# A band's side work in a scan layer: input rows scaled on GpSimd, and three pieces moved by a slot

## The chip, the cores and the metric

The kernel runs on one core of a Trainium2 chip. The metric is the device time of one execution in microseconds; of several runs the median is given.

## The reference, cut to what matters

The network has four layers on four images of 64 x 64 pixels and 128 channels. The change touches only the first layer, a selective scan in four directions. Cut to the parts that are spoken of:

```python
x = x + L0(_gn(x), ...)                       # group norm, then the layer
# L0:
xh, z = jnp.split(x @ in_proj_w.T, 2, axis=-1)   # 128 -> 2 x 256 channels
z  = silu(z)                                     # the "gates"
xc = silu(depthwise_conv_3x3(xh) + conv_b)
# four directions k over xc: delta, B, C from products of xc, then for each of 4096 positions
h = exp(delta * A) * h + (delta * u) * B         # 256 channels x 16 states
y = sum_n h[n] * C[n]
# the four results are added, and
y = layernorm(y) * out_norm_w + out_norm_b
return (y * z) @ out_proj_w.T
```

The group norm is a per-channel scale `s_` and offset `o_` for each image; "scaling the rows" means applying them to the input.

## The kernel before, in words

**Units and slots.** The first layer is a list of 128 units: 4 images x 4 directions x 8 chunks of 512 positions. A unit has 16 slots, one for each state `n` (the loop at L687). In every slot GpSimd forms `dB` (128 x 1024, L699), ScalarE two `dA` (128 x 512, L704), VectorE two scans `h` (L705), and `transposed()` (L536) gives TensorE eight transposes of an older unit's `h` into `pt` (L549) and eight products into `yT` (L584), and ScalarE the copy `hT` of `pt` (L559). The lag is seven slots. `pt` has one PSUM buffer, `dA` three, `dB` three. The order on TensorE, ScalarE, VectorE and GpSimd is the order in which the code issues (`manual_schedule`, L656); SyncE, which issues nearly all DMAs, is not in that list.

**Preparing the next unit.** `TABLE` (L612) puts the small steps that make the next unit's `delta` and `du` into slots 6 to 12: two products `dp`, four ScalarE passes, VectorE's `delta` (L484) in slots 9 and 11, and GpSimd's `du` (L487) in slots 10 and 12.

**Side work.** Beside the scan of one image, `before()` (L295) makes the next image's convolution and gates, and `after()` (L367) finishes the previous image. Both are generators; each `yield` names a need, and the loop at L741 lets a generator go on when the slot is in the need's set in `SIDE` (L626) and the piece is due. `later(place, f, slots=k)` puts an instruction into a place of the slot `k` slots on: "dve" ahead of the scans, "act0" and "act1" behind the first and the second scan, "act2" behind `hT`.

The side work of a band of 512 positions takes three units when convolutions are due. In this text they are called unit A, B and C:

- Unit A: the second gates' product `zp` in slot 1 (need "z"), its three ScalarE passes `e` in slots 2, 3 and 4, the product on VectorE in slot 5 (`silu`, L344). The previous image's product of `yg` and `z` on GpSimd in slot 7 (L414). The first convolution, nine taps of `cv` (L159), from slot 11 on, one tap a slot.
- Unit B: the convolution ends in slot 3, its passes are in 4, 5 and 6. The second convolution starts in slot 11. For `after()`, in the time of images 1 and 2 only, need "t" comes in slot 12 (`nb`, L388), the small product `mb` of 128 x 4 on VectorE in slot 14 (L390), and the four normalisations `yf` of 128 x 256 on ScalarE (L393) in slots 14 and 15 and in slots 0 and 1 of unit C. `xw`, a copy with transposed order (L362), is in slot 13.
- Unit C: the next band's rows `xn` (128 x 640) are scaled on ScalarE in slot 1 (L326, called by L341). The convolution ends in slot 3, its passes are in 4, 5 and 6. The band's transposes `pg` (L406, need "m") are in slots 11 and 12, their copies `yg` (L408) in 12 and 13, another `xw` in 13, the first gates' product `zp` in 13, and its passes in 14, 15 and in slot 0 of the next unit A.

`pg`, `zp`, `cv` and `dp` share one PSUM bank by way of `spare` (L501). In the time of image 0 there is no `after()`, so `mb`, `yf`, `pg` and `yg` are missing from the three units. In the time of image 3 there is no `before()`, and `after()` takes another form (need "n", normalisation on VectorE).

Of the kernel before, what the change touches and what calls it, by code (L numbers as in the profile page):

```python
# [12 lines left out]
AF = mybir.ActivationFunctionType  # L13
ALU = mybir.AluOpType
# [10 lines left out]
NCH = NT // CH  # L25
# [57 lines left out]
def layer0(sh, A, x_in, x_out, scr, ahead):  # L83
# [6 lines left out]
    tc, nc = sh.tc, sh.nc  # L90
    with ExitStack() as ctx:
# [76 lines left out]
        def grown(b, c, s, pm, later, e=None, gather=None):  # L168
            bias = conv_b[:, s : s + 1], conv_nb[:, s : s + 1]
            xo = silu(pm, *bias, scr(f"xr{b % 2}")[s, :, c * CH : (c + 1) * CH], later, (("act0", 2), ("act0", 3), 4), e)  # L170
            later("act0", gather or by_columns, xo, scr(f"xw{b % 2}")[s], c, slots=10)

        def gates(b, c, v, bank, later, es=(None, None)):
            for s in range(2):
                yield "z"
                zp = bank("zp")
                nc.tensor.matmul(zp, lhsT=w_in[:, 2 + s, :], rhs=v, start=True, stop=True)
                silu(zp, 0.0, 0.0, scr(f"z{b % 3}")[s, :, c * CH : (c + 1) * CH], later, (("act0", 2), ("act0", 3), 4), es[s])
# [126 lines left out]
        def before(b, bank, later):  # L305

            st = small.tile([P, NCH, 6], F32, name="gn_st")
            for c in range(NCH):  # L310
                yield "l"
                t = tmp.tile([P, CH], F32, name="xs", tag="t2", bufs=4)
                nc.sync.dma_start(t.rearrange("p (h w) -> p h w", w=64), A["x_t"][b, :, 8 * c + 1 : 8 * c + 9, 1:65])
                yield "s"
                later("dve", nc.vector.bn_stats, st[:, c, :], t)
            yield "m"
            s_, o_ = sh.group_scale(st, psm, small, "m", exp_rstd)

            def load(c):
                xn = tmp.tile([P, 10, 66], F32, name="xn", bufs=3)  # L320
                nc.sync.dma_start(xn, A["x_t"][b, :, 8 * c : 8 * c + 10, :])
                return xn

            def scaled(xn, c, r0, r1):
                inner = xn[:, max(r0, int(c == 0)) : min(r1, 10 - int(c == NCH - 1)), 1:65]
                nc.scalar.activation(inner, inner, AF.Identity, scale=s_, bias=o_)  # L326

            yield "l"
            ahead = load(0)
            yield "x"  # L330
            later("act2", scaled, ahead, 0, 0, 10)
            for c in range(NCH):
                xn = ahead
                yield from gates(b, c, xn[:, 1:9, 1:65], bank, later)
                for s in range(2):
                    for t, piece in enumerate(conv(xn, s, bank, out := [])):
                        yield piece
                        if c < NCH - 1 and (s, t) == (0, 0):
                            ahead = load(c + 1)
                        if c < NCH - 1 and s == 1 and t == 5:  # L340
                            later("act2", scaled, ahead, c + 1, 0, 10)  # L341
                    grown(b, c, s, out[0], later)

        def silu(v, bias, minus, dst, later, wait, e=None):  # L344
# [22 lines left out]
        def after(b, st, later, bands):  # L367

            for c in bands:
                yield "l"  # L370
                rows = slice(c * CH, (c + 1) * CH)
                if kept:
                    y = kept.pop()
                else:
                    y = tmp.tile([P, 4, 2 * P], F32, name="yf", tag="t4", bufs=4)
                    nc.sync.dma_start(y, tiles(scr(f"y2{b % 2}")[rows, :]))
                z = tmp.tile([P, 2, CH], F32, name="zf", tag="t4", bufs=4)
                nc.sync.dma_start(z, scr(f"z{b % 3}")[:, :, rows].rearrange("s p t -> p s t"))
                mv = small.tile([P, 4, 2], F32, name="ln_mv")
                for q in range(4):  # L380
                    nc.vector.bn_aggr(mv[:, q, :], st[:, 4 * c + q])

                rs = small.tile([P, 4], F32, name="ln_r")
                later("act1", nc.scalar.activation, rs, mv[:, :, 1], AF.Ln, bias=sh.eps5)
                if b + 2 < NB:
                    yield "t"
                    nb = small.tile([P, 4], F32, name="nb")
                    nc.scalar.activation(nb, rs, AF.Exp, scale=-0.5)  # L388
                    mb = small.tile([P, 4], F32, name="mb")
                    later("dve", nc.vector.scalar_tensor_tensor, mb, mv[:, :, 0], -1.0, nb, ALU.mult, ALU.mult, slots=2)  # L390
                    for q in range(4):
                        norm = dict(scale=nb[:, q : q + 1], bias=mb[:, q : q + 1])
                        later("act2", nc.scalar.activation, y[:, q, :], y[:, q, :], AF.Identity, slots=2 + q, **norm)  # L393
                else:
                    yield "n"

                    nb = spare("nb")[:, 0:4]
                    nc.scalar.activation(nb, rs, AF.Exp, scale=-0.5)
                    for q in range(4):
                        later("dve", normed, y[:, q, :], mv[:, q, 0:1], nb[:, q : q + 1])  # L400
                yg = tmp.tile([P, 2, CH], F32, name="yg", bufs=2)
                for s in range(2):
                    yield "m"
                    pt = spare("pg")
                    for q in range(4):
                        nc.tensor.transpose(pt[:, q * P : (q + 1) * P], y[:, q, s * P : (s + 1) * P], sh.ident)  # L406
                    norm = dict(scale=on_w[:, s : s + 1], bias=on_b[:, s : s + 1])
                    later("act0", nc.scalar.activation, yg[:, s, :], pt, AF.Identity, **norm)  # L408
                yield "f"
                xr = tmp.tile([P, 4, DM], F32, name="xr", tag="t2", bufs=4)  # L410
                nc.sync.dma_start(xr, tiles(x_in(b)[rows, :]))
                if b < NB - 1 or c > 2:
                    yield "g"
                nc.gpsimd.tensor_tensor(yg, yg, z, ALU.mult)  # L414
                if b + 2 < NB:
                    yield "o"
                    op = psy.tile([P, 2, 2 * P], F32, name=f"yT{int(not rev)}").rearrange("p r d -> p (r d)")
                else:
                    yield "m"
                    op = spare("op")  # L420
                op = op.rearrange("p (q d) -> p q d", q=4)
                for q in range(4):
                    for s in range(2):
                        nc.tensor.matmul(
                            op[:, q, :], lhsT=yg[:, s, q * P : (q + 1) * P], rhs=w_out[:, s, :], start=(s == 0), stop=(s == 1)
                        )
                later("dve", residual, b, rows, xr, op, slots=2)
# [134 lines left out]
        def products(G, q, hT):  # L562
# [61 lines left out]
            (12, "pool"): ("du1",),  # L624
        }
        SIDE = dict(  # L626
            m={0, 1, 2, 4, 5, 11, 12, 13, 14, 15},
            x={0, 1, 4, 5, 11, 12, 13, 14, 15},
            n={0, 1, 2, 3, 4, 11, 12, 14, 15},
            z={13, 1},  # L630
            c={11},
            g={7},
            s={11, 12, 13, 14, 15, 0, 1, 2, 3},
            t={11, 12, 15, 0},
            o={8},
            f=(),
            l=(),
# [3 lines left out]
        slot = 0  # L641

        def later(place, f, *a, slots=1, **kw):

            todo.setdefault((slot + slots, place), []).append(lambda: f(*a, **kw))  # L645
# [10 lines left out]
        with tc.manual_schedule(engines=order):  # L656
# [4 lines left out]
            for i, (b, k, c) in enumerate(units):  # L661
# [25 lines left out]
                for n in range(NS):  # L687
                    slot = NS * i + n
                    g, q = divmod(n, 4)
# [39 lines left out]
                    if n == 10:  # L729
                        y = unit["y"] = tmp.tile([P, 4, 2 * P], F32, name="y", tag="t4", bufs=4)  # L730
# [15 lines left out]
                        d.step()  # L746
                    for d in sides:
                        if d.need == "t" and n in SIDE["t"] and d.due(slot) and (inside or not any(o.taps for o in sides)):
                            d.free_at = slot + 6
                            d.step()  # L750
                        if d.need == "o" and n in SIDE["o"] and d.due(slot - 8):
                            d.step()
                        if d.need == "s" and n in SIDE["s"] and d.due(slot):
                            d.step()
                        if d.need in ("f", "l") and d.due(slot):
                            if d.need == "l":
                                d.free_at = slot + 3
                            d.step()
# [1455 lines left out]
```

## Time and profile before

| | |
|---|---|
| median of 3 runs | 7645.87 us (7638.12 to 7647.14) |
| the profiled execution's own time | 7645.85 us |
| its span from first to last instruction | 7644.1 us |
| mean granted TensorE clock | 0.966 |
| the scans of the first layer, from first to last | 112.8 to 5594 us |
| units of image 0, 1, 2, 3 begin at | 112.8, 1480.7, 2865.8, 4249.0 us |

The profile's page gives busy time by engine, the chain of waits that ended last, and groups of instructions by source line. In the timeline each row is one instruction or several merged ones: start, length, engine, line, operands, count, and in brackets the idle time of the engine just before and what ended it. Idle times below about 0.15 us are merged away. A row's length can overlap the next row's, since an engine starts its next instruction before the last has drained; the distance between two starts, the pitch, is what an instruction costs its engine.

### The profile page before, as it was taken

Reading aid. Unit: us, or ns where it says so; the run is one execution under the profiler, and the core shown is the slowest. Engines: PE = TensorE matmul, PEld = TensorE weight load, DVE = VectorE, ACT = ScalarE, POOL = GpSimd, SP = SyncE. Lnnn points to the kernel's source line nnn. Section 1 sums busy time; section 2 is a strip of 40 time slices with the busy share of each in tenths; the row PEclk is TensorE's granted clock in tenths of the full one; section 3 lists DMA queues with packets and bytes.
Section 4 is the critical chain, followed back from the end, with each engine's and each line's share of the span. In section 5 each row is a group of like instructions: output and inputs, shape, how many; then the busy total and the mean of one; then the engine's idle time right before and its main releaser. Section 6 shows DMA issues by size and latency. Waiting matters only on the chain.

```text
span 7644.1 us, 140402 instructions
## 1 busy us (share of the span) xinstructions
PE 6293.8 (82%) x52604; PEld 3973.6 (52%) x52604; DVE 6715.7 (88%) x7999; ACT 6135.0 (80%) x9771; POOL 5691.9 (74%) x2688
## 2 busy tenths in 40 slices
PE   7888888778898877888887777787789978686889
PEld 3554444444455544445554444454467756464556
DVE  7999999999999999999999999999956655656678
ACT  7999999999999999999999999999943323324667
POOL 4999999999999999999999999999920024123233
PEclk8999999999999999999999999999999988788999
DMA  6656566546667554565756445555533241331332
GB/s 181 171 177 176 182 175 180 171 154 178 198 180 195 184 179 160 167 196 178 183 191 180 165 169 180 179 185 174 190 92 73 59 120 46 83 99 46 102 95 82
DMA packets 1328925, 1160.66 MB, mean 152 GB/s; under 512 B 718709, under 2 KB 1119697, under 8 KB 1261298
## 3 DMA queue, kind: packets, MB, share of 16 engines
q1 hardware_dynamic: 1323970, 1149.24, 50.4%
q8 instruction: 414, 6.78, 0.4%
q10 hardware_dynamic: 4272, 2.43, 0.1%
q14 instruction: 269, 2.20, 0.1%
HBM read 958.19 MB, written 189.21 MB: 150 GB/s over the span
## 4 chain that ended last, share of the span: by engine, by line
ACT 36%; PE 31%; DVE 18%; issue 8%; POOL 3%; DMA 2%; SPq 1%; ACTq 0%; DVEq 0%; POOLq 0%
ACT hT L559 14%; ACT dA L704 14%; DVE h L705 12%; PE pt L549 5%; PE cv L159 3%; POOL dB L699 3%; PE yT L584 3%; PE pf L939 2%; PE po L952 1%; ACT e L645 1%; ACT delta L478 1%; PE yT L458 1%; PE pz L1183 1%; PE pt L1892 1%; ACT delta L481 1%
## 5 line engine op out<-in xcount | busy, mean ns | idle before, releaser
L705 DVE TENSOR_TENSOR_SCAN h<-dA,state,dB 128x512 f32<-128x512 f32 x4096 | 4927.0, 1266 | 120.7 <-ACT dA L704 72.4
L699 POOL TENSOR_TENSOR dB<-du,Bb 128x1024 f32<-128x1024 f32 x2048 | 4816.5, 2387 | 152.3 <-DVE h L705 118.2
L549 PE MATMUL pt<-ident,h 128*128 128x128 f32 x16384 | 2216.7, 278 | 859.2 <-ACT hT L559 833.8
L704 ACT ACTIVATE dA<-delta,A_neg 128x512 f32<-128x512 f32 x4096 | 2765.5, 696 | 102.7 <-DVE h L705 77.0
L549 PEld LDWEIGHTS pt<-ident,h 128*128 128x128 f32 x16384 | 1802.7, 141 | 1917.7 <-ACT hT L559 1700.5
L559 ACT COPY hT<-pt 128x1024 f32<-128x1024 f32 x2048 | 2080.7, 1016 | 125.5 <-PE pt L549 105.9
L584 PE MATMUL yT<-hT,W 128*32 128x256 f32 x16384 | 1378.6, 409 | 4.3 <-DVE xr L433 3.5
L584 PEld LDWEIGHTS yT<-hT,W 128*32 128x32 f32 x16384 | 456.2, 150 | 346.3 <-issue 324.3
L159 PE MATMUL cv<-xn,taps 128*128 128x512 f32 x936 | 527.1, 645 | 2.7 <-DVE delta L484 2.6
L1183 POOL TENSOR_TENSOR xg<-xg,so 128x1024 f32<-128x1024 f32 x16 | 39.3, 2469 | 622.8 <-PE pu L1183 622.2
L1930 POOL TENSOR_TENSOR S<-S,sm 128x784 f32<-128x784 f32 x128 | 191.1, 1493 | 416.3 <-DVE sm L1928 250.0
L487 POOL TENSOR_TENSOR du<-delta,u 128x512 f32<-128x512 f32 x256 | 327.8, 1281 | 163.6 <-DVE delta L484 162.2
L475 PE MATMUL dp<-xd,w_dt 65*128 65x512 f32 x512 | 288.7, 646 | 33.8 <-DVE delta L484 23.7
L458 PE MATMUL yT<-u,w_x 128*48 128x512 f32 x508 | 244.4, 604 | 21.3 <-DVE y L600 20.1
L1937 ACT ACTIVATE S<-S,mx 128x196 f32<-128x196 f32 x512 | 227.9, 448 | 33.2 <-DVE mx L1964 32.7
L159 PEld LDWEIGHTS cv<-xn,taps 128*128 128x128 f32 x936 | 139.2, 188 | 180.5 <-issue 160.4
L940 ACT ACTIVATE h<-pf,b 128x512 f32<-128x512 f32 x128 | 87.6, 687 | 118.8 <-PE pf L939 100.5
L484 DVE SCALAR_TENSOR_TENSOR delta<-delta,dp 128x512 f32<-128x512 f32 x256 | 169.7, 663 | 3.2 <-ACT delta L481 1.0
L1183 POOL TENSOR_TENSOR WX<-wr,Xs 128x544 f32<-128x544 f32 x40 | 59.3, 1483 | 149.1 <-issue 63.4
L1892 PE MATMUL pt<-ident,S 128*98 128x128 f32 x1024 | 165.6, 286 | 3.5 <-POOL S L1930 2.0
L481 ACT ACTIVATE delta<-delta 128x512 f32<-128x512 f32 x256 | 164.5, 643 | 0.0
L478 ACT ACTIVATE delta<-dp 128x512 f32<-128x512 f32 x256 | 152.3, 595 | 10.4 <-PE dp L475 9.2
(381 smaller groups left out, 6921.7 us busy)
## 6 DMA issues: line engine op xcount, KB each, us to landing
Bb<-l_B SPq DMA_DIRECT2D x512, 1024.0 KB
W<-l_W SPq DMA_DIRECT2D x512, 256.0 KB
l_y<-y SPq DMA_DIRECT2D x127, 512.0 KB
u<-l_xr SPq DMA_DIRECT2D x64, 512.0 KB
u<-l_xw SPq DMA_DIRECT2D x64, 512.0 KB
y<-l_y SPq DMA_DIRECT2D x56, 512.0 KB
V<-l_v SPq DMA_DIRECT2D x512, 49.0 KB
y<-l_y SPq DMA_DIRECT2D x80, 256.0 KB
```

Of the source, the lines that this page charges most:

```text
L159: nc.tensor.matmul(pm, lhsT=taps[:, s, t, :], rhs=xn[:, dy : dy + 8, dx : dx + 64], start=(t == 0), stop=(t == 8),)
L458: nc.tensor.matmul(bank["x"], lhsT=w_x[:, s, k, :], rhs=u[:, s, :], start=(s == 0), stop=(s == 1))
L475: nc.tensor.matmul(bank[s], lhsT=w_dt[:, k, s * P : (s + 1) * P], rhs=xd, start=True, stop=True)
L481: nc.scalar.activation(delta[:, s, :], delta[:, s, :], AF.Ln, bias=1.0)
L487: nc.gpsimd.tensor_tensor(du[:, s, :], delta[:, s, :], u[:, s, :], ALU.mult)
L549: nc.tensor.transpose(pt[:, j, s, :], G["h"][:, s, t0 : t0 + 32, :].rearrange("p t n -> p (t n)"), sh.ident)
L559: return lambda: nc.scalar.copy(hT, pt.rearrange("p j s d -> p j (s d)"))
L584: nc.tensor.matmul(U["yT"][e][32 * jo : 32 * jo + 32, qo % 2, :], lhsT=U["Ws"][G["g"]][:, :, 4 * q + j], rhs=hT[:, j, :], start=((e, jo) n ...
L699: nc.gpsimd.tensor_tensor(dB, du, B_now[:, q : q + 1, :].to_broadcast([P, 2, CH]), ALU.mult)
L704: nc.scalar.activation(dA, delta[:, s, :], AF.Exp, scale=A_neg[:, k, s, n : n + 1])
L705: nc.vector.tensor_tensor_scan(h[:, s, :, q], dA, dB[:, s, :], state[:, s, n : n + 1], ALU.mult, ALU.add)
L1892: nc.tensor.transpose(pt[:, half, hp, :], U["S"][:, e, hp, 98 * half : 98 * half + 98], sh.ident)
```

## The change

The scaling of a band's rows goes from ScalarE to GpSimd and from slot 1 of unit C to slot 8 of unit B, seven slots and one unit boundary earlier (`s == 0, t == 8` is reached in slot 3, and five slots are added). The scaling of an image's first band also goes to GpSimd. The small product and the four normalisations come one slot later (15, then 15, 0, 1, 2). Need "m" loses slot 11, so the transposes of unit C are in slots 12 and 13 and their copies in 13 and 14. The gates' products go from slots 13 and 1 to 14 and 2, and with them their passes and VectorE products. Need "t" keeps only slot 12, which is the one that it has now in the time of images 1 and 2, and its generator waits seven slots instead of six.

```diff
             def scaled(xn, c, r0, r1):
                 inner = xn[:, max(r0, int(c == 0)) : min(r1, 10 - int(c == NCH - 1)), 1:65]
-                nc.scalar.activation(inner, inner, AF.Identity, scale=s_, bias=o_)
+                nc.gpsimd.tensor_scalar(inner, inner, s_, o_, ALU.mult, ALU.add)
...
-                        if c < NCH - 1 and s == 1 and t == 5:
-                            later("act2", scaled, ahead, c + 1, 0, 10)
+                        if c < NCH - 1 and s == 0 and t == 8:
+                            later("act2", scaled, ahead, c + 1, 0, 10, slots=5)
...
-                    later("dve", nc.vector.scalar_tensor_tensor, mb, mv[:, :, 0], -1.0, nb, ALU.mult, ALU.mult, slots=2)
+                    later("dve", nc.vector.scalar_tensor_tensor, mb, mv[:, :, 0], -1.0, nb, ALU.mult, ALU.mult, slots=3)
...
-                        later("act2", nc.scalar.activation, y[:, q, :], y[:, q, :], AF.Identity, slots=2 + q, **norm)
+                        later("act2", nc.scalar.activation, y[:, q, :], y[:, q, :], AF.Identity, slots=3 + q, **norm)
...
-            m={0, 1, 2, 4, 5, 11, 12, 13, 14, 15},
+            m={0, 1, 2, 4, 5, 12, 13, 14, 15},
...
-            z={13, 1},
+            z={14, 2},
...
-            t={11, 12, 15, 0},
+            t={12},
...
-                            d.free_at = slot + 6
+                            d.free_at = slot + 7
```

## The prediction, made before the run

> **What bounds the kernel now.** I read the page first: the share of busy time, the chain, and the groups of the first layer.
>
> ```profile
> PE 6293.8 (82%) x52604; PEld 3973.6 (52%) x52604; DVE 6715.7 (88%) x7999; ACT 6135.0 (80%) x9771; POOL 5691.9 (74%) x2688
> ACT 36%; PE 31%; DVE 18%; issue 8%; POOL 3%; DMA 2%; SPq 1%; ACTq 0%; DVEq 0%; POOLq 0%
> L705 DVE TENSOR_TENSOR_SCAN h<-dA,state,dB 128x512 f32<-128x512 f32 x4096 | 4927.0, 1266 | 120.7 <-ACT dA L704 72.4
> L699 POOL TENSOR_TENSOR dB<-du,Bb 128x1024 f32<-128x1024 f32 x2048 | 4816.5, 2387 | 152.3 <-DVE h L705 118.2
> ```
>
> The chain names ScalarE and TensorE, but over the first layer VectorE is busy some 97% of the time (1346.6 of 1385 us in image 1's part, by the busy times by stretch). So VectorE's scans are the bound and the rest of the chain is what makes them wait. All that can be won lies in VectorE's idle time, mostly `h` waiting for `dA`. The waits of images 1 and 2 (1480 to 4250 us) say so:
>
> ```profile
> DVE h L705 <- ACT dA L704: 49.5, 97, 1.0
> POOL du L487 <- DVE delta L484: 77.6, 59, 2.1
> PEld zp L177 <- ACT yg L645: 13.8, 14, 1.0
> ```
>
> Next, ScalarE's and VectorE's timelines around the steps that move, in a band of image 1 (unit C from 2001.28 us):
>
> ```profile
> 2003.79 1.01 ACT L559 COPY hT<-pt 128x1024 f32<-128x1024 f32 x1
> 2004.69 0.61 ACT L645 ACTIVATE yf<-yf,mb,nb 128x256 f32<-128x256 f32 x1
> 2005.19 0.92 ACT L326 ACTIVATE xn<-xn,gn_o,gn_s 128x640 f32<-128x640 f32 x1
> 2006.01 1.30 ACT L704 ACTIVATE dA<-delta,A_neg 128x512 f32<-128x512 f32 x2
> ...
> 1995.19 1.45 DVE L645 SCALAR_TENSOR_TENSOR mb<-ln_mv,nb 128x4 f32<-128x4 f32 x1
> 2006.80 9.66 DVE L705 TENSOR_TENSOR_SCAN h<-dA,state,dB 128x512 f32<-128x512 f32 x8 [0.71 <-ACT dA L704]
> 2038.20 1.28 DVE L705 TENSOR_TENSOR_SCAN h<-dA,state,dB 128x512 f32<-128x512 f32 x1 [0.88 <-ACT dA L704]
> 2039.80 2.46 DVE L705 TENSOR_TENSOR_SCAN h<-dA,state,dB 128x512 f32<-128x512 f32 x2 [0.31 <-ACT dA L704]
> 2042.43 2.46 DVE L705 TENSOR_TENSOR_SCAN h<-dA,state,dB 128x512 f32<-128x512 f32 x2 [0.17 <-ACT dA L704]
> ```
>
> Two bursts make VectorE wait: the fourth `yf` together with `xn` in slot 1 (0.71), and `yg`, `xw`, `yg` in slots 12 and 13 (0.88, 0.31 and what follows). And `mb`, four elements wide, holds VectorE for 1.45 us.
>
> The pitches, from these timelines: two `dA` 1.22, `hT` 0.91, so a bare slot costs ScalarE 2.13 us; `yf` adds 0.50, `e` 0.50, `yg` 0.66, `xw` 0.97, `xn` 0.82. Two scans cost VectorE 2.35, a product beside them 0.58. TensorE with a tap of `cv` needs 2.53 a slot (`cv` begins at 2085.44 and 2087.97).
>
> Last, busy time by stretch. Columns: length, PE, PEld, DVE, ACT, POOL.
>
> ```profile
> 710.54:728.38 17.84, 17.01 (x127) 9.72 (x125) 16.85 (x14) 16.83 (x24) 17.84 (x8) 1.00 1.10 225
> 668.20:685.93 17.73, 16.90 (x127) 9.83 (x126) 17.11 (x15) 15.86 (x23) 17.73 (x8) 1.00 0.73 242
> 2126.09:2143.53 17.44, 15.91 (x114) 8.96 (x114) 16.69 (x16) 17.40 (x27) 16.44 (x8) 1.00 1.16 259
> 2160.68:2190.80 30.12, 22.17 (x196) 13.44 (x192) 28.30 (x26) 30.01 (x44) 28.94 (x15) 1.00 0.55 160
> ```
>
> The first is slot 14 of B to slot 5 of C in image 0's time, with `xn`; the second the same slots of A to B, without `xn`; the third is B to C in image 1, `xn` beside `yf`; the fourth slot 11 of C to slot 6 of A in image 1.
>
> **What the Trainium skill says.** "SBUF — State Buffer", Who interferes with whom: a VectorE instruction with two SBUF inputs and a GpSimd one that reads SBUF exclude each other for a whole instruction. `mb` fits: in all 16 cases it ends within 0.05 us of the end of the running `dB` in the two timelines. L430, also two SBUF inputs, takes 0.47 us beside a running `dB`, so the rule isn't general here. "ScalarE: Activation LUTs", What ACT_TABLE_LOAD costs: 186 + 0.833 N ns plus 93 per pointer operand, 93 overlapping; for N = 640 that is 0.81, and the pitch of `xn` is 0.82. "GPSIMD Engine Reference", 4.1 Engine selection: one-input work is roughly at line rate. In the trace a copy of 128 x 640 takes 0.84 us (L248), but TENSOR_SCALAR 3.01 us for 1024 elements.
>
> **The change part by part.**
>
> (1) `xn` leaves ScalarE. In image 0's time it is almost hidden: TensorE's nine taps need 2.53 a slot anyway. The stretch with it is 17.84, the one without 17.73, mean difference over five bands 0.11; with the waits around it I take 0.15. There are 7 such bands, and in images 1 and 2 two more without `yf` beside: 9 x 0.15 = 1.4 us. In 12 bands (six an image) `yf` stands beside it. There ScalarE is busy 17.40 of 17.44 and VectorE idles 0.75 to 1.16, mean 0.98. Afterwards ScalarE needs 2.63 in slots 15, 0, 1, 2 and 2.13 in slot 3. When the scans of slot 15 begin it is 0.7 ahead now; without the `yf` of slot 14 about 1.0, since TensorE's 2.53 takes part of the 0.5. Four slots at 2.63 - 2.35 = 0.28 use up 1.1, and slots 3 and 4 then wait for TensorE as they do in unit B. I leave 0.33 idle: 12 x 0.65 = 7.8 us.
>
> (2) `pg`, `yg`, `zp` and `e` one slot later. The same passes, but `xw` now meets the first `yg`, with the reserve of a free slot 12 behind it, and unit A's `e` begin in slot 3 instead of 2, so that slot 2 lets ScalarE recover. Slot by slot for image 1 from slot 12 of C to slot 5 of A, ScalarE's need against VectorE's plus its reserve: before 2.54, 3.76, 2.63, 2.65, 2.96, 2.37, 2.35, 2.61, 2.96, 2.96 (the distances between the scans' starts, mean of five bands, sum 27.8). After: 2.35, 3.26 (reserve 0.5 off 3.76), 2.79, 2.63, 2.65, 2.93, 2.35, 2.35, 2.63, 3.42, sum 27.4. So 0.4 less, in 14 bands: 5.6 us. In image 0's time only `zp` moves: 0.25 by the same count, 7 bands, 1.8 us. TensorE's new waits (the second `pg` for the first `yg`, one shared bank) end before the next `hT` would let it go on: `yg` ends 2.4 us into the slot, `pg` takes 0.66, `hT` ends at 3.8. Behind them stand `pt` and `zp`; without that cover, up to 1.0 us a band.
>
> (3) An image's first band: `zp` waited for `xn` in slot 1 (VectorE idle 0.37 and 0.47 at 1616.39 and 1618.14). With GpSimd ahead and `zp` a slot later I take 0.8 for images 1 and 2, 0.3 for image 0: 1.9 us.
>
> (4) `xn` on GpSimd. Price between 0.84 (the copy) and 1.88 us (3.01 x 640/1024); I take 1.88, the same operation. It stands behind `dB` of slot 8, ahead of two `dB` and `du`. There GpSimd waits anyway:
>
> ```profile
> 2105.18 2.38 POOL L699 TENSOR_TENSOR dB<-du,Bb 128x1024 f32<-128x1024 f32 x1 [0.28 <-DVE h L705]
> 2108.18 2.38 POOL L699 TENSOR_TENSOR dB<-du,Bb 128x1024 f32<-128x1024 f32 x1 [0.63 <-DVE h L705]
> 2111.91 1.28 POOL L487 TENSOR_TENSOR du<-delta,u 128x512 f32<-128x512 f32 x1 [1.34 <-DVE delta L484]
> ```
>
> That is 2.25 us, and 0.24 + 0.63 + 1.09 = 1.96 in image 0's bands. Cost nothing at both ends. Its rows were loaded tens of us before; SyncE's loads don't move with it. Without this cover each us would reach `dB` of slot 13, which is ready only 0.3 us ahead in image 0's time.
>
> (5) `mb` a slot later. It ends when GpSimd's `dB` ends, and GpSimd runs without gaps from `du` on, 2.34 a `dB` against VectorE's 2.35 a slot. So the scans of slot 15 begin at the same boundary as now: the wait of 1.35 us stays, bounds -0.3 and +0.3 x 16; I take 0. SyncE's stores of the gates follow their products by a slot; `W` loads behind them are used slots later: 0.
>
> (6) Image 3's `pg` and `op` from slot 11 to 12: TensorE idles 0.3 to 0.9 a slot there; 0, bounds -1.5 and +1.5.
>
> Sum: 1.4 + 7.8 + 5.6 + 1.8 + 1.9 = 18.5 us. The profiled execution took 7645.85 us, the median is 7645.87; so 7627.4, said as 7627.
>
> **Rivals.** *TensorE takes over* in the 12 bands too, as in image 0's: (1) gives 12 x 0.15 + 1.4 = 3.2, (2) half, 3.7, (3) 1.9: 7637. For it: 2.53 a slot under the taps. Against: TensorE idles 1.5 us in the third stretch. *GpSimd becomes late*: if the two scalar operations cost a pass each, `xn` takes 3.8; 1.8 too much in 7 bands (less 0.3 of lead) and 1.55 in 14, where `mb` passes the later boundary on in full: 10.5 + 21.7 = 32, so 7646 - 18.5 + 32 = 7659, slower. It decides from 1.96 us on. Against: the row of 3.01. *All of ScalarE's relief arrives*: half of the idle time that I leave in the 14 bands (1.83 - 0.4 + 0.33, half of it 0.9) goes too, 13 us more: 7614.
>
> **Chances.** Forecast 0.58 (7617 to 7637, terms half to one and a half), TensorE 0.20, GpSimd 0.12, all relief 0.10. A measurement of this kernel tells about 0.2%, 15.3 us, from no change; the forecast lies just beyond it, two thirds of its case faster (0.40), with the last case 0.50; TensorE and the other third 0.37 the same; slower 0.13 with some of it for mishaps. The range 7608 to 7645 leaves out the slow rival and little else.
>
> **What would show it.** Right: no `xn` on ScalarE, one of about 1.9 us on GpSimd ahead of a shortened wait of `du`; VectorE's wait in slot 1 of C gone, that in slot 13 still near 0.9; `mb` still ended by `dB`; units of image 3 unchanged. Wrong: `dB` late in slot 13, or `mb` of another length, since a changed phase between GpSimd and VectorE would outweigh the small terms.

## The result, and the profile after

| | before | after |
|---|---|---|
| median of 14 runs each | 7643.74 us (7638.12 to 7651.99) | 7630.74 us (7625.07 to 7634.70) |
| ratio, 95% interval | | 0.998 (0.9974 to 0.9987) |
| span of the profiled execution | 7644.1 us | 7630.5 us |
| the scans of the first layer end at | 5594.3 us | 5584.7 us |

The change makes the kernel 13 us faster by the medians. That is 0.17%, at the edge of what the prediction called measurable, though the interval leaves out a ratio of 1. The forecast was 18.5 us.

From the page of the changed kernel, the lines that answer to those shown of before: busy time, shares of the chain, the scans and `dB`.

```profile
PE 6285.6 (82%) x52604; PEld 3974.8 (52%) x52604; DVE 6715.5 (88%) x7999; ACT 6117.9 (80%) x9747; POOL 5707.3 (75%) x2712
ACT 38%; PE 35%; DVE 16%; issue 7%; POOL 2%; DMA 2%; SPq 1%; ACTq 0%; DVEq 0%; POOLq 0%
L705 DVE TENSOR_TENSOR_SCAN h<-dA,state,dB 128x512 f32<-128x512 f32 x4096 | 4927.8, 1266 | 113.7 <-ACT dA L704 60.8
L699 POOL TENSOR_TENSOR dB<-du,Bb 128x1024 f32<-128x1024 f32 x2048 | 4816.4, 2390 | 120.9 <-DVE h L705 91.1
```

ScalarE has 24 instructions fewer and GpSimd 24 more. The scans' wait for `dA` fell from 72.4 to 60.8 us. GpSimd's wait for `h` fell by 27.1, from 118.2 to 91.1 us; 24 rows at 0.88 us are 21 of that. What one of them costs GpSimd, from the instructions on the tile `xn` (least, median, most ns), and how it stands in slot 8 of a unit B, from GpSimd's timeline:

```profile
L326 POOL TENSOR_SCALAR xn<-xn,gn_s,gn_o x24: 822/880/972, 333.9 to 3864.8; 128x640 f32<-128x640 f32 x18, 128x576 f32<-128x576 f32 x6
```

```profile
1964.28 7.05 POOL L699 TENSOR_TENSOR dB<-du,Bb 128x1024 f32<-128x1024 f32 x3
1971.31 0.90 POOL L326 TENSOR_SCALAR xn<-xn,gn_s,gn_o 128x640 f32<-128x640 f32 x1
1972.15 4.78 POOL L699 TENSOR_TENSOR dB<-du,Bb 128x1024 f32<-128x1024 f32 x2
1978.27 1.28 POOL L487 TENSOR_TENSOR du<-delta,u 128x512 f32<-128x512 f32 x1 [1.33 <-DVE delta L484]
```

0.88 us in the median (0.90 in the mean of the 18 with 640 elements), not the 1.88 taken. The two waits of 0.28 and 0.63 ahead of `dB` are used up, and the wait of `du` for `delta` is still 1.33.

Next VectorE's timeline of the same band, from the end of unit B on; unit C begins at 1997.13, its slot 12 at 2028.78.

```profile
1993.59 1.25 DVE L645 SCALAR_TENSOR_TENSOR mb<-ln_mv,nb 128x4 f32<-128x4 f32 x1
1994.76 16.94 DVE L705 TENSOR_TENSOR_SCAN h<-dA,state,dB 128x512 f32<-128x512 f32 x14
...
2026.41 5.98 DVE L705 TENSOR_TENSOR_SCAN h<-dA,state,dB 128x512 f32<-128x512 f32 x5
2032.89 1.28 DVE L705 TENSOR_TENSOR_SCAN h<-dA,state,dB 128x512 f32<-128x512 f32 x1 [0.51 <-ACT dA L704]
2034.49 2.49 DVE L705 TENSOR_TENSOR_SCAN h<-dA,state,dB 128x512 f32<-128x512 f32 x2 [0.31 <-ACT dA L704]
2037.29 2.46 DVE L705 TENSOR_TENSOR_SCAN h<-dA,state,dB 128x512 f32<-128x512 f32 x2 [0.31 <-ACT dA L704]
2039.91 2.46 DVE L705 TENSOR_TENSOR_SCAN h<-dA,state,dB 128x512 f32<-128x512 f32 x2 [0.15 <-issue]
```

Fourteen scans now follow `mb` without a named wait; the 0.71 of slot 1 is gone. From slot 13 of C on, though, the waits are only spread out: 0.88, 0.31, 0.17 became 0.51, 0.31, 0.31, 0.15, in sum 1.36 before and 1.28 after. ScalarE's and VectorE's busy time in the two stretches of the next band (slot 14 of B to 5 of C, slot 11 of C to 6 of A; columns as in the prediction):

```profile
2119.94:2137.95 18.01, 17.00 (x127) 9.63 (x125) 17.84 (x15) 17.66 (x27) 17.60 (x8) 1.00 1.16 270
2155.11:2185.14 30.03, 22.02 (x196) 13.40 (x191) 28.34 (x26) 29.91 (x44) 29.18 (x15) 1.00 0.56 155
```

The first stretch holds `mb` now, so its length doesn't compare with the 17.44 of before. VectorE idles 0.17 in it (18.01 - 17.84) where it idled 0.75. The second is 0.09 shorter than the 30.12 of before.

**Where the time went.** The starts of the scans give the length of each part (us, difference to before):

| | image 0 | image 1 | image 2 | image 3 | later layers |
|---|---|---|---|---|---|
| before | 1367.9 | 1385.1 | 1383.2 | 1345.3 | 2049.8 |
| after | -1.2 | -7.9 | -6.0 | **+5.7** | -4.0 |

The later layers run the same instructions in every kernel here, and their part lay between 2038 and 2052 us in ten executions, one of each. So the 4.0 is no more than scatter, and the first layer gained 9.3: 15.0 in three images, less 5.7 lost in the fourth, where nothing was forecast.

### The profile page after: what moved, and what is told of

Read it like the earlier page. It is cut to its first block, busy times and chain, and to the rows that moved or that the text cites. A ratio compares the mean times of both kernels' runs of the same rounds, so it can differ in the third digit from the quotient of the medians.

```text
span 7630.5 us, 140452 instructions
## 1 busy us (share of the span) xinstructions
PE 6285.6 (82%) x52604; PEld 3974.8 (52%) x52604; DVE 6715.5 (88%) x7999; ACT 6117.9 (80%) x9747; POOL 5707.3 (75%) x2712
## 4 chain that ended last, share of the span: by engine, by line
ACT 38%; PE 35%; DVE 16%; issue 7%; POOL 2%; DMA 2%; SPq 1%; ACTq 0%; DVEq 0%; POOLq 0%
ACT hT L559 15%; ACT dA L704 14%; DVE h L705 9%; PE pt L549 6%; PE cv L159 4%; PE yT L584 3%; ACT e L645 2%; PE pf L939 2%; PE pz L1183 1%; PE po L952 1%; POOL dB L699 1%; PE yT L458 1%; ACT delta L478 1%; PE pt L1892 1%; ACT delta L481 1%
## 5 line engine op out<-in xcount | busy, mean ns | idle before, releaser
L705 DVE TENSOR_TENSOR_SCAN h<-dA,state,dB 128x512 f32<-128x512 f32 x4096 | 4927.8, 1266 | 113.7 <-ACT dA L704 60.8
L699 POOL TENSOR_TENSOR dB<-du,Bb 128x1024 f32<-128x1024 f32 x2048 | 4816.4, 2390 | 120.9 <-DVE h L705 91.1
```

The costliest lines, as they stand in the source:

```text
L699: nc.gpsimd.tensor_tensor(dB, du, B_now[:, q : q + 1, :].to_broadcast([P, 2, CH]), ALU.mult)
L705: nc.vector.tensor_tensor_scan(h[:, s, :, q], dA, dB[:, s, :], state[:, s, n : n + 1], ALU.mult, ALU.add)
```

## The experiments

Theory: the rows give the gain because they leave ScalarE; the other moves trade one wait for another; image 3's loss comes from slot 11 taken out of need "m". Rivals stand with each run. Each run's profile also gives a **band**: 48 slots from slot 5 of B to slot 5 of the next B, mean of the 14 of images 1 and 2, before 130.31 and after 129.55 us. (In image 0 the seven bands run from slot 5 of C to slot 5 of the next C: before 127.13, after 127.02.) Single bands repeat between executions to some 0.05 us, but for a single unit now and then, so this tells apart what medians can't. A stretch "slot 13 of B to slot 5 of C" goes from start to start.

**Slot 11 given back to image 3 alone.**

```diff
-            m={0, 1, 2, 4, 5, 12, 13, 14, 15},
+            m={0, 1, 2, 4, 5, 12, 13, 14, 15}, M={0, 1, 2, 4, 5, 11, 12, 13, 14, 15},
...
-                    yield "m"                              # ahead of pg
+                    yield "m" if b + 2 < NB else "M"
...
-                    yield "m"                              # ahead of op
+                    yield "M"
```

> The changed kernel, but the pieces of the previous image's finish may use slot 11 again in the time of image 3 (need M instead of m). Theory, lost cover: in image 3's time VectorE waits for GpSimd's dB in slot 13 whatever it does; the residual addition (0.58 us) used to lie in that wait and now, one slot later, lies outside. Undoing it there gives back 5.7 us in image 3's time (1335.8 us in the profile before, 1341.5 after) and nothing elsewhere: about 7625 us, ratio to before 0.9975. Rival, noise or DMA order: image 3's part stays within 1.5 us of the changed kernel's, 7630 us.

Measured: 7623.56 us, ratio 0.9971 (0.9960 to 0.9982). Image 3 is within 0.04 us of before (+5.7 in the changed kernel), the bands stay at 129.56. The loss is slot 11's. By the medians alone the two kernels aren't told apart (the intervals overlap); the trace does it. VectorE in unit 101, in slots 11 to 15, first of the changed kernel, then of this one:

```profile
4472.09 4.80 DVE L705 TENSOR_TENSOR_SCAN h<-dA,state,dB 128x512 f32<-128x512 f32 x4
4477.98 2.48 DVE L705 TENSOR_TENSOR_SCAN h<-dA,state,dB 128x512 f32<-128x512 f32 x2 [1.09 <-POOL dB L699]
4480.36 0.66 DVE L433 TENSOR_TENSOR xr<-xr,op 128x512 f32<-128x512 f32 x1
4480.94 3.63 DVE L705 TENSOR_TENSOR_SCAN h<-dA,state,dB 128x512 f32<-128x512 f32 x3
```

```profile
4471.55 4.81 DVE L705 TENSOR_TENSOR_SCAN h<-dA,state,dB 128x512 f32<-128x512 f32 x4
4476.27 0.67 DVE L433 TENSOR_TENSOR xr<-xr,op 128x512 f32<-128x512 f32 x1
4477.47 9.51 DVE L705 TENSOR_TENSOR_SCAN h<-dA,state,dB 128x512 f32<-128x512 f32 x8 [0.53 <-POOL dB L699]
```

With slot 11, VectorE's addition of the residual (L433) comes ahead of the scans of slot 13, where VectorE waits for `dB` anyway: 0.58 of work (the distance from 4480.36 to 4480.94) and 0.53 of wait. One slot later the wait is 1.09, and the addition comes after it, in full.

**That addition alone a slot later**, with slot 11 given back: its cover is taken away, TensorE's order is left.

```diff
-                later("dve", residual, b, rows, xr, op, slots=2)
+                later("dve", residual, b, rows, xr, op, slots=2 if b + 2 < NB else 3)
```

> The kernel with slot 11 given back to image 3, but with the residual addition of image 3's time still one slot later (slot 14 at the eight products that lie in slot 11). Theory, lost cover: the wait for dB in slot 13 stays and the addition comes on top: 5 us more in image 3's time than with slot 11 given back, as in the changed kernel, 7630 us. Rival, TensorE: it is the output product's 2.0 us in slot 12 that holds up the transposes; then image 3 keeps the time that slot 11 gives back, 7625 us.

Measured: 7629.76 us, ratio 0.9983 (0.9976 to 0.9990), image 3 +5.0. The loss is back with TensorE's pieces where they were, so it isn't TensorE. Its timeline shows the same picture as the changed kernel's:

```profile
4478.86 2.46 DVE L705 TENSOR_TENSOR_SCAN h<-dA,state,dB 128x512 f32<-128x512 f32 x2 [1.09 <-POOL dB L699]
4481.24 0.66 DVE L433 TENSOR_TENSOR xr<-xr,op 128x512 f32<-128x512 f32 x1
```

Slot 11 to slot 15 of the eight units with this wait takes 10.63 us in the mean before and with slot 11, 11.39 in the changed kernel, 11.23 here: 8 x 0.76 = 6.1 and 8 x 0.60 = 4.8, close to the 5.7 and 5.0 of the whole image. The difference between the two is a second instruction of VectorE. In five of the eight units the next band's statistics (L381, four small instructions, 0.27 us together) stand beside the addition. In the changed kernel they too come after the wait, and these units take 11.47 to 11.50; here they are ahead of it, as before, and all eight take 11.21 to 11.26. Unit 99 of the changed kernel is one of the five:

```profile
4393.57 2.46 DVE L705 TENSOR_TENSOR_SCAN h<-dA,state,dB 128x512 f32<-128x512 f32 x2 [1.10 <-POOL dB L699]
4395.95 0.35 DVE L381 BATCH_NORM_AGGREGATE ln_mv<-ln_st 128x2 f32<-128x6 f32 x4
4396.22 0.65 DVE L433 TENSOR_TENSOR xr<-xr,op 128x512 f32<-128x512 f32 x1
```

**Only the rows** (the kernel before, with the two edits at L326 and L341), and **everything but the rows** (the changed kernel, without them).

> The kernel before with nothing but the rows' scaling on GpSimd in slot 8 of unit B. Theory, ScalarE's relief: nearly all the gain of images 1 and 2 comes from this (12 bands x 0.65), image 0 gains 1, the first bands lose part of what they gained since the gates' product is still in slot 1; image 3 is as before. First layer 8 to 10 us shorter than before, 7634 us. Rival, the transposes and gates make the gain: first layer at most 3 us shorter, 7641 us.

> The changed kernel, but the rows are scaled on ScalarE in slot 1 of unit C as before; the transposes, gates and the small product are where the change puts them. Theory, ScalarE's relief: no gain in slots 0 to 3 of unit C (xn still meets a yf), 0.2 us a band from the transposes and gates in 14 bands, and the loss of 5.7 in image 3: first layer 1 to 4 us longer than before, 7646 us. Rival, the transposes and gates make the gain: first layer 5 us or more shorter than before, 7638 us.

Measured: only the rows 7630.05 us, ratio 0.998 (0.9972 to 0.9988), bands 129.57. Everything but the rows 7647.40 us, ratio 1.0002 (0.9993 to 1.0010), bands 130.28. The rows alone are the whole gain of the change, 0.74 a band: images 0 to 2 together are 15.1 us shorter with them, and 15.0 in the changed kernel. The rest gives 0.03 a band and loses 5.7 in image 3. (Images 0 to 2 are 4.4 shorter with it, but not in the bands; 2.2 of that is image 1's first band, which scatters nearly as much, see step 3 below.) By its trace the kernel with only the rows is 14.2 us shorter than before in the first layer, more than the 8 to 10 expected, and as short as the one with slot 11 (14.1). Their medians, from the same session, still lie 6.5 us apart, so a distance of that size between medians decides nothing here. VectorE around slots 14 of B to 5 of C, of the kernel with only the rows and of the one without them:

```profile
1990.42 1.45 DVE L645 SCALAR_TENSOR_TENSOR mb<-ln_mv,nb 128x4 f32<-128x4 f32 x1
1991.80 19.08 DVE L705 TENSOR_TENSOR_SCAN h<-dA,state,dB 128x512 f32<-128x512 f32 x16
```

```profile
1993.96 1.27 DVE L645 SCALAR_TENSOR_TENSOR mb<-ln_mv,nb 128x4 f32<-128x4 f32 x1
1995.15 7.15 DVE L705 TENSOR_TENSOR_SCAN h<-dA,state,dB 128x512 f32<-128x512 f32 x6
2002.94 2.46 DVE L705 TENSOR_TENSOR_SCAN h<-dA,state,dB 128x512 f32<-128x512 f32 x2 [0.64 <-ACT dA L704]
```

Sixteen scans without a named wait, against 0.64 at the end of slot 1 and another 0.17 after it.

**Is it the engine or the slot?** The changed kernel with the rows on ScalarE in slot 8 of B, and with the rows on GpSimd in slot 1 of C, where they were.

```diff
-                nc.gpsimd.tensor_scalar(inner, inner, s_, o_, ALU.mult, ALU.add)
+                nc.scalar.activation(inner, inner, AF.Identity, scale=s_, bias=o_)
```

```diff
-                        if c < NCH - 1 and s == 0 and t == 8:
-                            later("act2", scaled, ahead, c + 1, 0, 10, slots=5)
+                        if c < NCH - 1 and s == 1 and t == 5:
+                            later("act2", scaled, ahead, c + 1, 0, 10)
```

> The changed kernel, but the rows are scaled on ScalarE, in slot 8 of unit B. It tells the engine from the slot. Theory, ScalarE is short in slot 8 too: 0.82 us more on ScalarE, of which the 0.49 us that it idles in slot 9 takes part in images 1 and 2, none in image 0's time; 7 x 0.8 + 14 x 0.4 = 11 us more than the changed kernel, 7642 us. Rival, only slot 1 of unit C was short: within 2 us of the changed kernel, 7631 us.

> The changed kernel, but GpSimd scales the rows in slot 1 of unit C. It tells the slot from the engine. Theory: GpSimd takes 0.88 us for it; in images 1 and 2 it is 2.4 us ahead of the scans there and idles after it, so nothing changes; in image 0's time it is 1.1 us ahead, and stays ahead; within 2 us of the changed kernel, 7631 us. Rival, slot 8 matters because du waits there: each of the 7 bands of image 0 loses 0.6 us, those of images 1 and 2 up to 0.9, together 4 to 17 us, 7635 to 7648 us.

Measured: ScalarE in slot 8 7645.60 us, ratio 1.0002 (0.9994 to 1.0011); its bands are 129.88, and those of image 0 are 127.68 where the changed kernel has 127.02. GpSimd in slot 1 7629.07 us, ratio 0.9983 (0.9976 to 0.9990), its bands those of the changed kernel to 0.06 us, but for one with a unit 2.4 us longer. On GpSimd, then, no slot had to be chosen. On ScalarE the slot does matter, and slot 8 is no free place. Compared with the rows on ScalarE in slot 1 (everything but the rows), slot 8 wins 0.40 a band in images 1 and 2 (130.28 to 129.88), more than half of the 0.73 that GpSimd wins there, and loses 0.51 a band in image 0 (127.17 to 127.68). With single units counted in, the first layer ends at 5595.0 us against 5595.2. So the slot alone moves the loss to another image, and the gain of the whole needs the other engine. In slot 1 GpSimd has no wait to hide the rows in, and still nothing is late:

```profile
1987.78 7.07 POOL L699 TENSOR_TENSOR dB<-du,Bb 128x1024 f32<-128x1024 f32 x3
1994.84 0.87 POOL L326 TENSOR_SCALAR xn<-xn,gn_s,gn_o 128x640 f32<-128x640 f32 x1
1995.68 16.41 POOL L699 TENSOR_TENSOR dB<-du,Bb 128x1024 f32<-128x1024 f32 x7
```

In this profile image 3 lost 9.9 us instead of 5.7, though its code there is that of the changed kernel; units 104, 108 and 116 are 0.3, 1.0 and 2.7 longer. Why stays open.

**The small product on GpSimd**, with slot 11 given back. `mb` holds VectorE 1.1 us a band in the changed kernel's mean, since it ends when the running `dB` does. Here it is two small GpSimd instructions in slot 14, and VectorE has none.

```diff
-                    later("dve", nc.vector.scalar_tensor_tensor, mb, mv[:, :, 0], -1.0, nb, ALU.mult, ALU.mult, slots=3)
+                    later("dve", minus_mean, mb, mv, nb, slots=2)
...
+        def minus_mean(mb, mv, nb):
+            nc.gpsimd.tensor_tensor(mb, mv[:, :, 0], nb, ALU.mult)
+            nc.gpsimd.tensor_scalar(mb, mb, -1.0, None, ALU.mult)
```

> The kernel with slot 11 given back to image 3, and the small product mb on GpSimd (a product and a multiplication by -1) in slot 14 instead of on VectorE in slot 15, so that VectorE no longer waits for GpSimd's running dB. Theory, the wait is a cover: during the 0.7 to 1.2 us that mb holds VectorE, ScalarE catches up from xw; without it VectorE waits for dA instead, and a band gains only the 0.35 us that ScalarE idles there: 14 x 0.35 = 5 us less than the kernel with slot 11 given back, 7620 us. Rival, the wait is a pure loss: its whole length goes, 16 x 1.1 = 17 us less, 7608 us.

Measured: 7626.53 us, ratio 0.9973 (0.9963 to 0.9983), bands 129.61 and 129.56 in the two images, as without it (129.56). Nothing is won, neither the theory's 5 us nor the rival's 17, though the two cost GpSimd under 0.5 us and VectorE's 1.1 are gone. Its timelines, GpSimd's first:

```profile
1990.35 0.19 POOL L430 TENSOR_TENSOR mb<-ln_mv,nb 128x4 f32<-128x4 f32 x1
1990.64 0.22 POOL L431 TENSOR_SCALAR mb<-mb 128x4 f32<-128x4 f32 x1
1990.82 9.42 POOL L703 TENSOR_TENSOR dB<-du,Bb 128x1024 f32<-128x1024 f32 x4
```

```profile
1984.23 12.01 DVE L709 TENSOR_TENSOR_SCAN h<-dA,state,dB 128x512 f32<-128x512 f32 x10
1996.68 2.46 DVE L709 TENSOR_TENSOR_SCAN h<-dA,state,dB 128x512 f32<-128x512 f32 x2 [0.44 <-issue]
1999.32 2.46 DVE L709 TENSOR_TENSOR_SCAN h<-dA,state,dB 128x512 f32<-128x512 f32 x2 [0.18 <-ACT dA L708]
2001.95 2.46 DVE L709 TENSOR_TENSOR_SCAN h<-dA,state,dB 128x512 f32<-128x512 f32 x2 [0.17 <-ACT dA L708]
2004.59 7.32 DVE L709 TENSOR_TENSOR_SCAN h<-dA,state,dB 128x512 f32<-128x512 f32 x6 [0.17 <-ACT dA L708]
```

Four waits of 0.44, 0.18, 0.17 and 0.17 stand where `mb` stood, three of them for `dA` (for the first the profile names nothing). These waits read as follows: while `mb` held VectorE, ScalarE got ahead with its `dA`; without it ScalarE, with a `yf` in each of these slots, is the later one.

**The normalisations in their old slots**, with slot 11 given back: `mb` in 14, `yf` in 14, 15, 0 and 1.

```diff
-mb, mv[:, :, 0], -1.0, nb, ALU.mult, ALU.mult, slots=3)
+mb, mv[:, :, 0], -1.0, nb, ALU.mult, ALU.mult, slots=2)
...
-AF.Identity, slots=3 + q, **norm)
+AF.Identity, slots=2 + q, **norm)
...
-                            d.free_at = slot + 7
+                            d.free_at = slot + 6
```

> The changed kernel with slot 11 given back to image 3, and with the small product and the four normalisations in the slots of the kernel before (14, then 14, 15, 0, 1); the rows on GpSimd and the gates' products in their new slots. Theory (the later normalisations were not needed and leave a pass in slot 2, where ScalarE has no reserve): slots 13 of B to 5 of C of a band in image 1 fall from 20.72 to 20.53, slot 2 of C from 2.59 to 2.37, slots 11 of C to 6 of A stay at 30.03, the twelve bands of images 1 and 2 together 2 to 3 us shorter than with slot 11 alone, median about 7621. Rival (the later normalisations are what gives the later transposes their room, so the two belong together): slots 11 of C to 6 of A go back from 30.03 to 30.12 or above, and the median stays at 7623 to 7625.

Measured: 7621.73 us, ratio 0.9972 (0.9961 to 0.9983). Slot 13 of B to slot 5 of C is 20.53 (20.72), slot 2 of C 2.37 (2.59), both as the theory said. Slot 11 of C to slot 6 of A has a mean of 30.14 in the four typical bands, which is the rival's number, but from one unit alone: it is 30.39 there, and 30.04 to 30.06 in the other three, against 30.03. So the transposes don't need the later normalisations. The whole band falls only from 129.56 to 129.43, though, over 14 bands 1.8 us, less than the 2 to 3 expected. This kernel and the one with slot 11 alone have the lowest two medians, both ahead of before and (by the trace) of the changed kernel; the medians don't tell them apart.

## Why the prediction was right, and where not

The predicted time was 7627 us and the measured one 7630.74, inside the range. The direction and its main reason, the rows' relief of ScalarE, were right, but two terms were wrong: step 2 won far less than forecast, and step 6 lost time where nothing was forecast. By its own steps:

- **(1) The rows leave ScalarE.** Right, in mechanism and size. In the typical bands of image 1, slot 13 of B to slot 5 of C fell from 21.36 to 20.72: 0.64, forecast 0.65. Alone, the rows gave 0.83 there, their whole pitch on ScalarE (0.82; the 0.81 that the prediction worked out from the Trainium skill is an estimate). Of the 0.33 that the working left idle, 0.19 came from the normalisations' later slots, as the last run shows. In image 0 the same stretch fell by 0.17, forecast 0.15: there TensorE's taps hide the rows, which cost 0.66 on ScalarE where no taps stand beside them (slot 8). *TensorE takes over* gave 0.15 to all bands and is refuted by 0.64 and by the kernel with only the rows.
- **(2) The gates' products and transposes a slot later.** Mis-sized, and this is the term that took most from the sum: 0.4 a band was forecast, and 0.09 measured (30.12 to 30.03), over 14 bands 1.3 us instead of 5.6. Of the ten distances between slots, the sum was to fall from 27.8 to 27.4 and fell from 27.75 to 27.66. Slot 13 of C came to 3.37 instead of 3.26: the empty slot 12 gave ScalarE a reserve of 0.38 and not of the 0.5 counted. Slot 5 of A came to 3.55 instead of 3.42: with slot 2 free, slots 3 to 5 took 8.51 before and after, so "recovery" in slot 2 was worth nothing, where 0.11 was counted. The rest is 0.06, net, in the other eight slots. Image 0's stretch got 0.08 longer instead of 0.25 shorter. TensorE's new wait came as described (below) and delayed nothing that shows.
- **(3) First bands.** 48 slots from the start of units 4, 34 and 66 fell by 0.2, 1.4 and 0.9, together 2.5; forecast 1.9. But at unit 34 the same code was 0.6 us longer than before in one execution (slot 11 given back) and 1.4 shorter in two, and the rows alone gave 3.2 in all, with `zp` where it was. So this is agreement in size only.
- **(4) The rows on GpSimd.** Cost nothing, as forecast, at half the price taken: 0.88 us, beside the copy of 0.84 and not 3.01 x 640/1024. The Trainium skill's "GPSIMD Engine Reference", 4.1 Engine selection, one-input work at about line rate, agrees here with the copy and with this row (the 3.01 for 1024 elements doesn't fit it). The point of decision at 1.96 us was far off, and the rows in slot 1 of C show that not even the wait for `delta` was needed as a cover. *GpSimd becomes late* is refuted.
- **(5) `mb` a slot later.** Right: 0. Slot 13 of B to slot 15 takes 6.05 us before and 6.01 after; `mb` ends with the running `dB`, as the skill's "SBUF — State Buffer", Who interferes with whom, lets one expect of two SBUF inputs, at 0.78 to 1.96 us a piece. The prediction held L430 against that rule, wrongly: in the kernel before, the factor `nb` of L430 lies in PSUM (L397, by way of `spare`), so only one of its two tensors is in SBUF, and its 0.47 us beside a running `dB` is no exception. What the prediction called a wait that stays turned out to be a cover: removing it won nothing.
- **(6) Image 3's pieces from slot 11 to 12.** This step failed: 0 with bounds of 1.5 us was forecast, and 5.7 lost. It looked at TensorE alone. The edit also moves what follows each `op`: VectorE's addition two slots behind it, which had stood in VectorE's wait for `dB`, and in five units the statistics of the next band (L381). The addition alone, one slot later, lost 5.0.

*All of ScalarE's relief arrives* (7614) is refuted as well: ScalarE is still what slots 13 and 14 of C wait for. That wait (70.7 before), and TensorE's, by the list of waits between 200 and 5400 us (total, times, longest):

```profile
POOL du L487 <- DVE delta L484: 134.4, 113, 2.1
...
DVE h L705 <- ACT dA L704: 59.5, 171, 0.9
...
PEld pg L406 <- ACT yg L645: 15.9, 16, 1.0
```

`zp`'s wait for `yg` is gone and `pg`'s has taken its place, of the same size as the 13.8 shown before. A wait changed its name.

The sum of the first layer: 14 bands at 0.76 (10.6), 7 bands of image 0 at 0.11 (0.8), first bands 2.5, what is left in single units 1.1, less 5.7: 9.3 us. The measured ratio, 0.9974 to 0.9987, is 10 to 20 us, so the medians' 13.0 are 3.7 more than the first layer shows. The later layers' scatter, 14 us from least to most, is wide enough for that; more isn't known. The range, 7608 to 7645, took in every gain from 1 to 38 us, and that the median came within 4 us of 7627 is in part luck: the medians' 3.7 and single units made up for a part of what steps 2 and 6 lacked.

## What to carry to other kernels

When a bounding engine waits, an instruction inside that wait is free, and moving it by one slot can cost its full length: follow a moved step to the last instruction that it triggers, on every engine. Here relief of the busy engine paid where it took work out of it; moving passes about within it gave back in one slot, or in another image, what it won. And by the trace the one small edit, the rows alone, did as well as the whole change with slot 11 given back: try the parts before the sum. A long instruction that stalls the bounding engine may be what lets the next one keep up, so ask what would be late without it before removing it.

## What the runs showed of the hardware that was not expected

- GpSimd's scaling by two per-partition operands took 0.90 us in the mean for 128 x 640, though a row of the same name took 3.01 us for 128 x 1024 in a later layer; what makes the difference was not tried.
- The product of 128 x 4 took VectorE 0.78 to 1.96 us beside a running `dB`, and GpSimd 0.20 us plus 0.22 for the sign.
